# Block 0 of a two-block network as one hand-ordered TensorE stream, with expert weights spread by DMA and rotary tables made earlier

## The chip, the cores and the metric

The kernel runs on one core of a Trainium2 chip. The metric is the device time in microseconds (us) of one execution. A core has a matrix engine (PE, TensorE), three engines for elementwise work (DVE or VectorE, ACT or ScalarE, POOL or GpSimd), an engine whose queue only issues transfers here (SP), and DMA engines that move data between memory (DRAM) and the on-chip buffer. PE writes into a small accumulator memory, PSUM. Each engine takes its instructions in the order in which the program holds them, and an instruction waits on semaphores for what others must have done.

## The reference

Four batches (b) of 1024 tokens with 128 features go through two blocks; each has an attention part and a feed-forward part, both with a layer norm whose scale and shift come from a small conditioning product.

```
x = L0_attn_x                                           # 4 x 1024 x 128
sa, ca, ga, sb, cb, gb = split(silu(c0) @ wmod0)        # ga, gb kept at least 0.25 from 0
h = layernorm(x) * (1 + ca) + sa
q = softmax(heads(h Wq + bq)) * s;  k = softmax over tokens(q) * s;  v = heads(h Wv + bv)
x = x + ga * ((q @ (k^T v)) Wo + bo)                    # 16 heads of 8: linear attention
h = layernorm(x) * (1 + cb) + sb
score = sigmoid(h gate_w)                               # 16 experts in 4 groups
comb  = score, kept for the best 4 experts of the best 2 groups (score + gate_bias), else 0
x = x + gb * (sum_e comb_e * (silu(h w1_e) * (h w3_e)) w2_e + shared expert)
h = layernorm(x) * (1 + ca1) + sa1
x = x + ga1 * windowed_attention(h)                     # window 64, 16 global prefix keys
h = layernorm(x) * (1 + cb1) + sb1
for l in 0, 1:                                          # inner layers: l2-normed q and k,
    h = h + local_attention(rotary(qk-scaled h)) wo     # rotary with a scale per position,
    h = h + gelu_mlp(layernorm(h))                      # window 64, 8 heads of 64
x = x + gb1 * h
```

Each expert has 64 hidden features, so that two of them fill the 128 rows of PE. All is float32 but some constants.

## The kernel before

Activations are kept with features on the 128 partitions and tokens along the free dimension: `xT[b]` and `hT[b]` are 128x1024 for each batch. Work goes in halves of a batch (k, 512 tokens)[...].

Block 0 is written as stages, each for all batches: norms h0 (line 194), the linear attention (`linear`, lines 256 to 312), norms h1 (325), the experts (354 to 419). Block 1 follows: norms h2 (426), the windowed attention (called attention 2 here), norms h3 (646), the two inner layers with their MLPs (656 to 880), and the output. In a stage, `staggered` (line 48) runs units as generators: each new unit begins while those before it go on to their next `yield`. The order of the instructions in these stages is set by a scheduler that the kernel's framework runs over them. In attention 2 and in the attention of the inner layers the order on PE alone is the one written (`manual_schedule`); the order on the other engines is the scheduler's there too. Tiles are drawn from pools with a number of buffers per tag; a new tile waits for the readers of the one whose buffer it takes.

A layer norm (lines 139 to 163) turns four 128x128 pieces to tokens on partitions (PE transposes, tile in_h), takes statistics on DVE (bn_stats, bn_aggr), makes the inverse root on POOL (add, pow), normalizes on DVE (xh), turns back (out_h) and scales and shifts on ACT into hT.

`route(b)` (354 to 377) is the gate: 8 products of 128x16 on PE, sigmoid on ACT, then ranks by counting. `rank` (337) compares every pair of values: two DVE operations, two POOL operations (128x2048 for the experts, eq_e and gt_e) and a DVE reduction; comb, 128 tokens x 8 x 16, comes out. A route is issued before batch 0's experts and, for the next batch, ahead of the second half of each batch.

`experts` (379 to 407) is one expert pair of one half: two products h1 and h3 into PSUM (388, 390), silu on ACT (u), a product on DVE (g), then the combination weights. Those lie with tokens on partitions, but are needed along the free dimension, on all 64 rows of an expert: POOL copies them 64 times each (ce, line 399), four PE transposes turn them (cw, 402), and DVE multiplies (403). The second stage adds the pair to y in PSUM (405). A ninth unit for each half is the shared expert, with 64 rows.

The rotary tables `ab` of an inner layer are `tab` (cosines and sines with scales, 1 MB, loaded at the start) times that layer's q and k scales: eight POOL operations at the top of each layer (lines 666 to 680), before `shifted` (648 to 654) and the projections qk (692); sums with ab follow on DVE (697, 702) and POOL (709).

Transfers are issued on SP's queue, some constants on ACT's. x of batches 0 and 1 is loaded first, that of 2 and 3 while the norms h0 run, then the weights of block 0, tab and the layers' weights.

Of the kernel before, what the change touches and what calls it, by code (L numbers as in the profile page):

```python
# [19 lines left out]
F32 = mybir.dt.float32  # L20
BF16 = mybir.dt.bfloat16
AF = mybir.ActivationFunctionType
# [4 lines left out]
P = 128  # L27
# [31 lines left out]
def adaln_blocks(ctx: ExitStack, tc: tile.TileContext, a: dict, out: bass.AP):  # L59
# [21 lines left out]
    xp = ctx0.enter_context(tc.tile_pool(name="xin", bufs=2))  # L81
# [23 lines left out]
    load_x(1)  # L105
# [33 lines left out]
    def layernorm(pp, wp, src, dst, scale, bias, name, tokens=None):  # L139


        tp = tokens
        if tp is None:
            tp = pp.tile([P, 4, D], F32, tag="ln", name=f"in_{name}")
            for i in range(4):
                pe.transpose(tp[:, i, :], src[:, i * P : (i + 1) * P], ident)
# [8 lines left out]
        yield  # L155
# [3 lines left out]
        yield  # L159
        tq = pp.tile([P, BLK], F32, tag="ln", name=f"out_{name}")  # L160
# [4 lines left out]
    def ln_all(src, jscale, jbias, m, pp, wp, name, before=None, tokens=None):  # L165
        hs = [hp.tile([P, N], F32, tag=f"hT{b}", name=f"{name}{b}") for b in range(B)]

        def units():
            for b in range(B):
                for k in range(NB):  # L170
                    s = slice(k * BLK, (k + 1) * BLK)
                    if before is not None:
                        before(b, k)
                    yield layernorm(
                        pp, wp, src[b][:, s], hs[b][:, s], m[:, jscale, b : b + 1], m[:, jbias, b : b + 1], f"{name}_{b}_{k}",
                        tokens[b][:, 4 * k : 4 * k + 4, :] if tokens else None,
                    )

        staggered(units())
        return hs  # L180


    m = mods[0]
    with tc.tile_pool(name="p0", bufs=4, space=PSUM) as pp, tc.tile_pool(name="w0", bufs=3) as wp:

        def to_features(b, k):
            if k == 0 and b + 2 < B:
                load_x(b + 2)
            tp = pp.tile([P, BLK], F32, tag="tr", name=f"xtr_{b}_{k}")
            for i in range(4):  # L190
                pe.transpose(tp[:, i * P : (i + 1) * P], xin[b][:, 4 * k + i, :], ident)
            dve.tensor_copy(xT[b][:, k * BLK : (k + 1) * BLK], tp)

        hT = ln_all(xT, 1, 0, m, pp, wp, "h0", to_features, xin)
# [14 lines left out]
    ws2 = const0("ws2", [INTER, D])  # L209
    nc.sync.dma_start(out=ws2, in_=a["ws2"])  # L210
# [5 lines left out]
    tab = const("tab", [P, 2, NT, 2, DH])  # L216
    nc.sync.dma_start(out=tab, in_=a["tab"])
    wl = []
    for l in range(DEPTH):
        w = [const(f"wqkv_{l}", [P, 3, HEADS * DH]), const(f"wo_{l}", [P, 4, D]), const(f"w1_{l}", [P, 2 * HID]), const(f"w2_{l}", [P, 3, D])]  # L220
        nc.sync.dma_start(out=w[0], in_=a["wqkv"][l].rearrange("p (i c) -> p i c", i=3))
        nc.sync.dma_start(out=w[1], in_=a["wo"][l].rearrange("(c p) d -> p c d", p=P))
        nc.sync.dma_start(out=w[2], in_=a["mw1"][l])
        for j, r in enumerate(CH):
            nc.sync.dma_start(out=w[3][:r, j, :], in_=a["mw2"][l][j * P : j * P + r, :])
        wl.append(w)
# [19 lines left out]

    s_attn = float((8.0**0.5) ** -0.25)
    with (
        tc.tile_pool(name="p1a", bufs=2, space=PSUM) as pqv,
        tc.tile_pool(name="p1b", bufs=2, space=PSUM) as pmid,  # L250
        tc.tile_pool(name="p1c", bufs=2, space=PSUM) as pctx,
        tc.tile_pool(name="w1a", bufs=3) as wp,
    ):
        gabo = const("gabo", [P, B])
        dve.tensor_scalar(gabo, m[:, 2, :], cols[:, V_BO : V_BO + 1], None, ALU.mult)
        def linear(b, k, qT, cps):
            nm = f"{b}_{k}"
            ps = pqv.tile([P, 4, 2, D], F32, tag="qv", name=f"qv_{nm}")
            for i in range(4):
                t = 4 * k + i  # L260
                pe.matmul(ps[:, i, :, :], lhsT=hT[b][:, t * P : (t + 1) * P], rhs=wqv, start=True, stop=True)
            q = wp.tile([P, 4, D], F32, tag="q", name=f"q_{nm}")
            dve.tensor_tensor(q, ps[:, :, 0, :], rows[:, R_BQ : R_BQ + D].unsqueeze(1).to_broadcast([P, 4, D]), ALU.add)
            v = wp.tile([P, 4, D + 1], F32, tag="v", name=f"v_{nm}")
            pool.memset(v[:, :, D : D + 1], 1.0)
            dve.tensor_tensor(v[:, :, 0:D], ps[:, :, 1, :], rows[:, R_BV : R_BV + D].unsqueeze(1).to_broadcast([P, 4, D]), ALU.add)
# [5 lines left out]
            yield  # L272
# [5 lines left out]
            ek = wp.tile([P, 4, D], F32, tag="ek", name=f"ek_{nm}")  # L278
            act.activation(ek, q, AF.Exp)
            yield  # L280
            tp = pmid.tile([P, BLK], F32, tag="mid", name=f"qtr_{nm}")
            for i in range(4):
                pe.transpose(tp[:, i * P : (i + 1) * P], q[:, i, :], ident)
            act.copy(qT[:, k * BLK : (k + 1) * BLK], tp)
# [7 lines left out]
            cx = wp.tile([P, H0, 8], F32, tag="cx", name=f"cx_{b}")  # L292
            dve.tensor_scalar(cx, cps[:, 0:D].rearrange("p (h e) -> p h e", e=8), rs, s_attn, ALU.mult, ALU.mult)
            dve.tensor_tensor(cx, cx, bc(hm16, [P, H0, 8]), ALU.mult)
            yield
            tp = pmid.tile([P, BLK], F32, tag="mid", name=f"cxtr_{b}")
            pe.transpose(tp[:, 0:P], cx.rearrange("p h e -> p (h e)"), ident)
            cxT = wp.tile([P, D], F32, tag="cxT", name=f"cxT_{b}")
            act.copy(cxT, tp[:, 0:P])
            yield  # L300
            mps = pmid.tile([P, BLK], F32, tag="mid", name=f"mps_{b}")
            pe.matmul(mps[:, 0:D], lhsT=cxT, rhs=wo0, start=True, stop=True)
            mo = wp.tile([P, D], F32, tag="mo", name=f"mo_{b}")
            act.copy(mo, mps[:, 0:D])
            yield
            for n in range(NB):
                s = slice(n * BLK, (n + 1) * BLK)
                ops = pmid.tile([P, BLK], F32, tag="mid", name=f"o0_{b}_{n}")
                pe.matmul(ops, lhsT=mo, rhs=qT[:, s], start=True, stop=True)
                og = wp.tile([P, BLK], F32, tag="og", name=f"og_{b}_{n}")  # L310
                act.activation(og, ops, AF.Identity, bias=gabo[:, b : b + 1], scale=m[:, 2, b : b + 1])
                pool.tensor_tensor(xT[b][:, s], xT[b][:, s], og, ALU.add)

        def linear_units():
            for b in range(B):
                qT = wp.tile([P, N], F32, tag="qT", name=f"qT0_{b}")
                cps = pctx.tile([P, D + 1], F32, tag="ctx", name=f"ctx_{b}")
                for k in range(NB):
                    yield linear(b, k, qT, cps)

        staggered(linear_units())


    with tc.tile_pool(name="p2", bufs=4, space=PSUM) as pp, tc.tile_pool(name="w2a", bufs=3) as wp:
        hT = ln_all(xT, 4, 3, m, pp, wp, "h1")

    with (
        tc.tile_pool(name="p3", bufs=1, space=PSUM) as pgate,
        tc.tile_pool(name="p4", bufs=2, space=PSUM) as pp,
        tc.tile_pool(name="p4y", bufs=1, space=PSUM) as py,  # L330
        tc.tile_pool(name="w3", bufs=2) as wr,
        tc.tile_pool(name="w4", bufs=3) as wp,
    ):
        triE = tri[:, 0 : E * E].unsqueeze(1).to_broadcast([P, NT, E * E])
        triG = tri[:, E * E :].unsqueeze(1).to_broadcast([P, NT, NG * NG])
# [16 lines left out]
        combs = {}  # L352

        def route(b):

            lg = pgate.tile([P, NT, E], F32, tag="gate", name=f"gate_{b}")
# [18 lines left out]
            cb = wr.tile([P, NT, E], F32, tag="comb", name=f"comb{b}")  # L375
            dve.scalar_tensor_tensor(cb, re, float(TOPK), so, ALU.is_lt, ALU.mult)
            combs[b] = cb

        def experts(b, k, c, y):

            s = slice(k * BLK, (k + 1) * BLK)
            nm = f"{b}_{k}_{c}"
            shared = c == E // 2
            r = INTER if shared else P
            wa = ws13[:, 0, :] if shared else w1[:, c * P : (c + 1) * P]
            wb = ws13[:, 1, :] if shared else w3[:, c * P : (c + 1) * P]
            h1 = pp.tile([P, BLK], F32, tag="h1", name=f"h1_{nm}")
            pe.matmul(h1[:r], lhsT=wa, rhs=hT[b][:, s], start=True, stop=True)  # L388
            h3 = pp.tile([P, BLK], F32, tag="h3", name=f"h3_{nm}")
            pe.matmul(h3[:r], lhsT=wb, rhs=hT[b][:, s], start=True, stop=True)  # L390
            u = wp.tile([P, BLK], F32, tag="u", name=f"u_{nm}")
            act.activation(u[:r], h1[:r], AF.Silu)  # L392
            g = wp.tile([P, BLK], F32, tag="g", name=f"g_{nm}")
            dve.tensor_tensor(g[:r], u[:r], h3[:r], ALU.mult)  # L394
            if not shared:
# [5 lines left out]
                for i in range(4):  # L401
                    pe.transpose(cw[:, i * P : (i + 1) * P], ce[:, i, :, :].rearrange("p j e -> p (j e)"), ident)  # L402
# [641 lines left out]
```

## Time and profile before

| what | value |
|---|---|
| median of three runs | 1627.3 us (1626.57 to 1628.82) |
| profiled execution, its time and its span | 1627.76 us, 1626.0 us |
| mean TensorE clock granted | 0.923 of full |
| PE busy in the span | 1411.2 us (87%) |
| DVE, POOL, ACT busy | 994.8, 691.8, 646.7 us (61, 43, 40%) |
| first qv product; first y product of an expert; end of the last | 45.7; 159.8; 397.6 us |
| first scores of attention 2 read by DVE | 441.96 us |
| start of inner layers 0 and 1 (qk) | 791.5; 1207.05 us |

The profile is of one execution. A row of groups names line, engine, operation, tiles written and read, shape and count; after the bar, busy time and mean duration in ns; after the second bar, how long the engine had been idle just before these instructions, and what ended that. A timeline row gives start and length in us, and the idle time before it in square brackets. The time of an execution is a little above its span, since it also covers what lies around the recorded instructions. Ends of products on PE are modelled, so that neighbours seem to overlap: the distance between starts is the safer measure.

### The profile page before, as it was taken

To read this page: it belongs to the slowest core of one execution; us is meant where nothing else is said; L and a number is where in the kernel's file an instruction comes from. 1 tells how busy PE (TensorE), PEld (TensorE's weight loads), DVE (VectorE), ACT (ScalarE), POOL (GpSimd) and SP (SyncE) were. 2 spreads that over 40 slices of the span, in tenths; PEclk is the share of its full clock that TensorE was granted. 3 is DMA by queue.
4 is the path that set the end of the run, shared out by engine and by line. 5 is a ranking of instruction groups with operands and counts; after the bars stand their busy time and mean duration, and the time that the engine had idled before them with its cause. 6 is when DMAs were issued, how large, how long until landed. Compare 5 with 4: busy or idle time off the path is not lost. (4 is left out here: it accounts for less than half of the span.)

```text
span 1626.0 us, 34277 instructions
## 1 busy us (share of the span) xinstructions
PE 1411.2 (87%) x14132; PEld 857.4 (53%) x14132; DVE 994.8 (61%) x2258; ACT 646.7 (40%) x1395; POOL 691.8 (43%) x715
## 2 busy tenths in 40 slices
PE   4857899898699999998589999997968999998797
PEld 3634344444366767776356666664325666665433
DVE  5754844544445555554578787765447878777563
ACT  1423111211122222222176767763216767767322
POOL 2344721411402021201677777762047777777110
PEclk8966899999589999998599999998989999999899
DMA  7000000000000000000011111110001111111001
GB/s 239 22 1 1 0 0 1 1 1 0 1 2 3 3 2 3 3 3 2 0 28 31 28 29 30 25 34 4 0 1 28 24 32 27 28 31 27 11 1 52
DMA packets 24241, 30.84 MB, mean 19 GB/s; under 512 B 3243, under 2 KB 15125, under 8 KB 23957
## 3 DMA queue, kind: packets, MB, share of 16 engines
q1 hardware_dynamic: 22788, 27.10, 6.7%
q8 instruction: 112, 1.84, 0.5%
q10 hardware_dynamic: 1296, 1.54, 0.3%
q14 instruction: 45, 0.36, 0.1%
HBM read 10.56 MB, written 2.10 MB: 8 GB/s over the span
## 5 line engine op out<-in xcount | busy, mean ns | idle before, releaser
L709 POOL TENSOR_TENSOR co<-co,si 128x512 f32<-128x512 f32 x128 | 162.6, 1271 | 110.2 <-DVE si L702 110.2
L708 POOL TENSOR_TENSOR ss<-ss,nhalf 128x16 f32<-128x16 f32 x64 | 188.6, 2946 | 5.3
L772 ACT ACTIVATE pr<-s,mx,ss 128x128 f32<-128x128 f32 x512 | 186.6, 486 | 0.0
L695 ACT ACTIVATE sq<-qk 128x512 f32<-128x512 f32 x128 | 79.8, 623 | 187.2 <-issue 140.8
L692 PE MATMUL qk<-wqkv,hs_a 128*128 128x512 f32 x256 | 142.3, 645 | 8.1 <-POOL hs_a L651 7.2
L719 PE MATMUL qktr<-ident,co 128*128 128x128 f32 x512 | 82.0, 283 | 52.9 <-POOL co L711 48.2
L392 ACT ACTIVATE u<-h 128x512 f32<-128x512 f32 (+1 forms) x72 | 42.8, 596 | 193.9 <-PE h L388 188.6
L560 ACT ACTIVATE pt<-t 128x384 f32<-128x384 f32 x128 | 55.8, 488 | 156.5 <-PE t L557 156.5
L524 DVE TENSOR_REDUCE mx<-s 128x4 f32<-128x448 f32 x128 | 70.9, 616 | 74.2 <-PE s L521 74.2
L491 POOL COPY hr<-h 128x512 f32<-128x512 f32 x32 | 19.5, 613 | 217.7 <-PE vp L494 217.7
L399 POOL COPY ce<-comb 128x512 f32<-128x512 f32 x64 | 46.6, 733 | 152.7 <-PE cw L402 147.1
L767 DVE TENSOR_REDUCE mx<-s 128x4 f32<-128x512 f32 x128 | 82.4, 685 | 38.5 <-PE s L763 38.2
L697 DVE TENSOR_TENSOR co<-qk,ab 128x512 f32<-128x512 f32 x128 | 87.0, 679 | 30.0 <-ACT sq L695 24.3
L780 PEld LDWEIGHTS ptr<-ident,pr 128*128 128x128 f32 x512 | 63.5, 142 | 63.2 <-issue 50.4
L394 DVE TENSOR_TENSOR g<-u,h 128x512 f32<-128x512 f32 (+1 forms) x72 | 49.0, 683 | 74.0 <-PE h L390 70.3
L162 PE MATMUL out_h<-ident,xh_h 128*128 128x128 f32 x128 | 45.2, 436 | 53.5 <-DVE xh_h L158 50.6
L719 PEld LDWEIGHTS qktr<-ident,co 128*128 128x128 f32 x512 | 57.7, 142 | 64.1 <-POOL co L711 56.2
L702 DVE TENSOR_TENSOR si<-qk,ab 128x512 f32<-128x512 f32 x128 | 87.0, 680 | 0.9 <-POOL ab L680 0.9
L704 DVE TENSOR_REDUCE ss<-sq 128x8 f32<-128x512 f32 x128 | 86.4, 675 | 0.0
L793 PE MATMUL o<-ve,pt 128*64 128x65 f32 x1024 | 86.1, 228 | 0.0
L793 PE MATMUL o<-vs,pt 128*64 128x65 f32 x1024 | 86.1, 228 | 0.0
L405 PE MATMUL y<-g,w 128*128 128x512 f32 x128 | 72.8, 659 | 14.7 <-DVE g L403 14.7
(227 smaller groups left out, 3322.3 us busy)
## 6 DMA issues: line engine op xcount, KB each, us to landing
ve<-vs SPq DMA_DIRECT2D x120, 130.0 KB, 2.3
xin<-in_x SPq DMA_DIRECT2D x4, 512.0 KB, 4.3
out<-out SPq DMA_DIRECT2D x8, 256.0 KB, 2.4
w<-in_w SPq DMA_DIRECT2D x3, 512.0 KB, 7.5
wqkv<-in_wqkv SPq DMA_DIRECT2D x2, 768.0 KB, 6.1
tab<-in_tab SPq DMA_DIRECT2D x1, 1024.0 KB
wmod<-in_wmod ACTq DMA_DIRECT2D x1, 768.0 KB
w<-in_mw SPq DMA_DIRECT2D x2, 341.0 KB, 5.6
```

Of the source, the lines that this page charges most:

```text
L405: pe.matmul(y, lhsT=ws2 if shared else w2[:, c, :], rhs=g[:r], start=(c == 0), stop=shared)
L692: pe.matmul(ps, lhsT=kept[b, "h"][:, t * P : (t + 1) * P], rhs=wqkv[:, w, :], start=True, stop=True)
L695: act.activation(sq, ph, AF.Square)
L697: dve.tensor_tensor(co, ph, ab[:, 0, t, w, :].unsqueeze(1).to_broadcast([P, HEADS, DH]), ALU.mult)
L702: dve.tensor_tensor(si.rearrange("p h (i e) -> p h i e", i=2), ex, sn, ALU.mult)
L704: dve.tensor_reduce(ss[:, w, :], sq, AX.X, ALU.add)
L708: pool.tensor_tensor(ss, ss, nhalf[:, 0:2].unsqueeze(2).to_broadcast([P, 2, HEADS]), ALU.pow)
L709: pool.tensor_tensor(co, co, si, ALU.add)
L719: pe.transpose(tp[:, i, :], co[:, i * P : (i + 1) * P], ident)
L767: dve.tensor_reduce(mx[:, j, :], S[j], AX.X, ALU.max, negate=True)
L772: act.activation(pr[:, c, :], S[j][:, c, :], AF.Exp, bias=mx[:, j, c : c + 1], scale=rq[:, j, c : c + 1])
L793: pe.matmul(o[qs, c, :], lhsT=pt[:, c, qs], rhs=vv[:, 2 * c + j, :], start=True, stop=True)
```

## The change

Block 0 becomes one stage whose PE order is written by hand (`manual_schedule`). Its work is cut into steps: `first(b)` is norm h0, qv and context of a batch (12 steps), `second(b)` the rest of the linear attention, norm h1 and route (9), `third(b)` norm h2 of block 1 (4). `first(0)`, then `second(0)` alternating with `first(1)`, run ahead; then, for each batch, its 16 expert pairs run with side steps among them: `third` of the batch before, `second` of the next and `first` of the one after, 21, 25, 13 and 4 steps in batches 0 to 3, dealt out evenly. The products with w2 (`mixed`) follow two pairs behind (`hidden`). PSUM is shared by tags: t (transposes and all side products) with two buffers, s (hidden products) with four, m and o one each.

`spread(b, k)` replaces the copies and transposes of the combination weights: four PE transposes of comb, a copy on ACT, a 16x512 write to DRAM, and 16 DMAs of one row each, repeated into 64 partitions (128 KB written by each). They are on SP's queue. The weights are then multiplied into u on POOL, ahead of DVE's product with h3. The shared expert of a batch is done with both halves in the two halves of the partitions. The copies into xT move from DVE to ACT; all of x is loaded at the start; qv is done in quarters.

The layers' weights (4 MB) and tab are now loaded after block 0, into memory that it gives back; tab lies in a pool of attention 2, and is issued first. The two rotary tables are made in attention 2, called at its sixth step (t == 5) of batches 1 and 2. As built, POOL's order has all these 16 operations (lines 506 to 514) between the add and pow of batch 3's norm h2, ahead of attention 2's first copies of hT (hr, 583) and of its first masked keys (kg, kx, 560 and 563). tab's transfer waits for the last y product of block 0, since it takes over memory of that block.

```diff
-    xp = ctx0.enter_context(tc.tile_pool(name="xin", bufs=2))
+    xp = ctx0.enter_context(tc.tile_pool(name="xin", bufs=4))
...
-            dve.tensor_copy(xT[b][:, k * BLK : (k + 1) * BLK], tp)
...
-    tab = const("tab", [P, 2, NT, 2, DH])
-    nc.sync.dma_start(out=tab, in_=a["tab"])
...
+        tc.manual_schedule(engines={mybir.EngineType.PE}),
...
+        def mid(name, shape=(P, BLK)):
+            return ps.tile(list(shape), F32, tag="t", name=name, bufs=2)
...
+            act.copy(xT[b][:, blk(k)], tp)
...
+        def spread(b, k):
+
+            tp = mid(f"combtr_{b}_{k}")
+            for i in range(4):
+                pe.transpose(tp[0:E, i * P : (i + 1) * P], kept[b, "comb"][:, 4 * k + i, :], ident)
+            ct = wb.tile([E, BLK], F32, tag="ct", name=f"ct_{b}_{k}")
+            act.copy(ct, tp[0:E, :])
+            cd = dr.tile([E, BLK], F32, tag="cd", name=f"cd_{b}_{k}")
+            nc.sync.dma_start(out=cd, in_=ct)
+            cw = kept[b, k, "cw"] = wc.tile([P, E // 2, BLK], F32, tag="cw", name=f"cw_{b}_{k}", bufs=2)
+            for e in range(E):
+                j = e % 2 * INTER
+                nc.sync.dma_start(out=cw[j : j + INTER, e // 2, :], in_=cd[e : e + 1, :].partition_broadcast(INTER))
...
-                ce = wp.tile([P, 4, 2, INTER], F32, tag="ce", name=f"ce_{nm}")
-                w = combs[b][:, 4 * k : 4 * k + 4, 2 * c : 2 * c + 2]
-                pool.tensor_copy(ce, bc(w, [P, 4, 2, INTER]))
-                cw = pp.tile([P, BLK], F32, tag="cw", name=f"cw_{nm}")
-                for i in range(4):
-                    pe.transpose(cw[:, i * P : (i + 1) * P], ce[:, i, :, :].rearrange("p j e -> p (j e)"), ident)
-                dve.tensor_tensor(g, g, cw, ALU.mult)
...
+            act.activation(u, hh[0], AF.Silu)
+            pool.tensor_tensor(u, u, kept[b, k, "cw"][:, c, :], ALU.mult)
+            g = kept[b, k, c, "g"] = wp.tile([P, BLK], F32, tag="g", name=f"g_{nm}")
+            dve.tensor_tensor(g, u, hh[1], ALU.mult)
...
+        def first(b):
+
+            r = [(norm0, b, 0), (features, b, 0), (norm0, b, 1), (norm_out, b, 0, "h0", m, 1, 0), (features, b, 1)]
+            r += [(qv, b, 0, 0), (norm_out, b, 1, "h0", m, 1, 0), (qv, b, 0, 1), (qv, b, 1, 0), (qv, b, 1, 1)]
+            return r + [(context, b, 0), (context, b, 1)]
+
+        def second(b):
+
+            r = [(turn_context, b), (join_context, b), (attended, b, 0), (attended, b, 1)]
+            r += [(norm_in, b, 0, "h1"), (norm_in, b, 1, "h1"), (norm_out, b, 0, "h1", m, 4, 3), (norm_out, b, 1, "h1", m, 4, 3)]
+            return r + [(route, b)]
...
+        run(first(0))
+        run(braid(second(0), first(1)))
+        for b in range(B):
+            side = third(b - 1) if b else []
+            if b + 1 < B:
+                side = side + second(b + 1)
+            if b + 2 < B:
+                side = side + first(b + 2)
+            if b == 0:
+                for k in range(NB):
+                    run([(spread, b, k)])
+            units = [(k, c) for k in range(NB) for c in range(E // 2)]
+            shared_hidden(b)
+            for i in range(len(units) + 2):
+                if i < len(units):
+                    hidden(b, *units[i])
+                take = max(0, (i + 1) * len(side) // len(units) - i * len(side) // len(units)) if i < len(units) else 0
+                at = i * len(side) // len(units)
+                run(side[at : at + take])
+                if i >= 2:
+                    mixed(b, *units[i - 2])
+                if i == len(units) - 1 and b + 1 < B:
+                    spread(b + 1, 0)
+            if b + 1 < B:
+                spread(b + 1, 1)
+        run(third(B - 1))
...
+        tab = wb.tile([P, 2, NT, 2, DH], F32, tag="tab", name="tab", bufs=1)
+        nc.sync.dma_start(out=tab, in_=a["tab"])
...
+            if t == 5 and 0 < b <= DEPTH:
+                rotary(tab, abs_[b - 1], b - 1)
...
-            ab = wt.tile([P, 2, NT, 2, DH], F32, tag="ab", name=f"ab_{l}")
...
+            ab = abs_[l]
```

## The prediction

> **What bounds the kernel now.** I first read the page's second part, its PE and PEclk rows: 40 slices of 40.65 us.
>
> ```profile
> PE   4857899898699999998589999997968999998797
> PEclk8966899999589999998599999998989999999899
> ```
>
> PE holds the kernel nearly everywhere; the loose slices are the first four, the eleventh (406 to 447 us) and the starts of later norms. The change touches the first eleven and the two layer starts (slices 20 and 30). So next come the busy times by stretch:
>
> ```profile
> core 0: us, PE busy (x) PEld busy (x) DVE busy (x) ACT busy (x) POOL busy (x), PEclk, DMA share, GB/s
> ...
> 100.00:150.00 50.00, 36.22 (x130) 23.66 (x130) 28.52 (x101) 15.48 (x20) 18.84 (x19) 0.63 0.00 1
> 150.00:200.00 50.00, 37.59 (x113) 19.59 (x114) 39.31 (x48) 7.50 (x11) 32.35 (x24) 0.82 0.00 0
> ...
> 250.00:300.00 50.00, 50.00 (x157) 22.45 (x155) 21.75 (x32) 9.92 (x17) 9.20 (x15) 1.00 0.00 1
> ...
> 400.00:450.00 50.00, 30.30 (x155) 15.75 (x155) 24.42 (x98) 7.57 (x11) 21.16 (x32) 0.56 0.00 0
> ```
>
> Where the experts run undisturbed (250 to 300 us) PE is full at full clock, with DVE at 44% and POOL at 18%. Around them it has holes, and works at a lowered clock. The timeline of PE there prices an expert unit:
>
> ```profile
> 253.60 0.60 PE L402 MATMUL cw<-ident,ce 128*128 128x128 f32 x4
> 254.04 1.02 PE L388 MATMUL h<-h,w 128*128 128x512 f32 x2
> 254.90 1.02 PE L390 MATMUL h<-h,w 128*128 128x512 f32 x2
> 255.76 1.02 PE L405 MATMUL y<-g,w 128*128 128x512 f32 x2
> 256.62 0.60 PE L402 MATMUL cw<-ident,ce 128*128 128x128 f32 x4
> ```
>
> From start to start: a 512-column product 0.86 us, four transposes 0.44, a unit 3.02. The hole before the experts, in the groups of 127 to 160 us:
>
> ```profile
> L345 POOL TENSOR_TENSOR eq_e<-eq_e,tri 128x2048 f32<-128x2048 f32 x1 | 6.5, 6498 | 5.7 <-DVE eq_e L342 5.7
> L347 POOL TENSOR_TENSOR gt_e<-gt_e,eq_e 128x2048 f32<-128x2048 f32 x1 | 4.5, 4493 | 0.1
> L360 ACT ACT_TABLE_LOAD x3 | 3.8, 1283 | 10.7 <-DVE comb L376 6.9 <-PE gate L358 3.8
> L349 DVE TENSOR_REDUCE rank_e<-gt_e 128x128 f32<-128x2048 f32 x1 | 2.3, 2285 | 4.5 <-POOL gt_e L347 4.5
> ```
>
> A batch's routing is a serial chain over POOL and DVE, 22 us from sigmoid (done 133.2) to comb (154.96); sigmoid and silu take turns in ACT's table, 1.283 a load. Last, the layer starts:
>
> ```profile
> 798.49 0.69 DVE L697 TENSOR_TENSOR co<-qk,ab 128x512 f32<-128x512 f32 x1 [5.34 <-POOL ab L680]
> 1207.05 5.49 PE L692 MATMUL qk<-wqkv,hs_a 128*128 128x512 f32 x6 [7.18 <-POOL hs_a L651]
> ```
>
> Both wait for POOL's rotary products: eight of 128x256 at 0.726, four of 128x512 at 1.488, four at 1.666, so 18.4 us in both layers.
>
> **What the Trainium skill says.** "Perfetto Trace Analysis", Optimization Strategy, advises interleaving regimes whose busiest engine differs; the table above has such regimes. "TensorE: Matmul & The Clock Gate", What's actually happening: the clock halves after an idle window of about 3.4 us and needs a busy one to recover; in the trace h passes lasted 0.96 us at 131 us and start 0.43 apart at 250, so every stall costs more than its length. "GPSIMD Engine Reference", 4.1 Engine selection: two-input elementwise work is about twice as slow there; POOL took 1.271 for 128x512, DVE 0.683.
>
> **The change, part by part.**
>
> *PE's work.* Block 0 after: 128 hidden products x 0.855 = 109.4; 64 mixed = 54.7; shared 16+8 = 20.5; eight kinds of transposes (x, two of each norm except h0's input, q, comb), 32 of each at 0.107 = 27.4; qv, context, o0 and gate 31. Together 243 us. Before it was 267: the 256 cw transposes cost 27.4, the new comb transposes 3.4. Before, this work and its holes took from 18.3 us to the first scores' maximum at 441.96. The gain is bounded by the holes.
>
> *The start.* Only batch 0's norms stand ahead of its first qv: about 23 us instead of 45.7. Softmax, context, o0 and two h1 norms are a serial chain of one batch (each half: stats 1.2, aggregate 0.6, POOL add and pow 1.26, xh 1.6, transposes 0.5, Identity 0.78, and hand-overs); gate(0) ends near 57, sigmoid 58. Routing takes the same 22: comb at 80 (155 before). Then, new: four transposes and a copy 1.1, the write to DRAM and the first broadcast, two DMAs on end. For these the nearest row is ve, 130 KB, 2.3 us to landing; with issue 7.4 in all, and a POOL product, so the first g is at 90. By unit 3 PE is warm: 96.
>
> *Spread weights.* Per unit it removes 4 transposes (0.44 PE), a POOL copy (0.733) and a DVE product (0.686), and adds a POOL product of 1.27 between silu and g. POOL has 64 x 0.54 = 34 us more in all, in a block where it was 18 to 65% busy: hidden, except when a rank block stands ahead on POOL. The 128 broadcasts (128 KB each, 16.8 MB) have one half's expert time, 8 x 2.57 + side work, about 30 us, per 2 MB. "SBUF — State Buffer", Door 1, has 196 GB/s measured for 64 partitions, so an estimate of 10.7 us per half; no run here shows it. Bounds: 0 (hidden) to 128 x what exceeds 1.9 us each. I take 0, since comb is ready well ahead for batches 1 and 2.
>
> *Batches.* Experts, shared and comb transposes are 47 PE us per batch; first(b) is 7.7, second 4.5, third 1.7. From t=96: batch 0, rest of it 50 plus stalls 15; batch 1, 60 plus 17.5; batch 2, 53 plus 24.6; batch 3, 45. The last y ends near 360. The stalls: PE is now one written order, so any late side step stops the experts too. The q softmax (reduce, subtract on POOL, exp, sum, reciprocal, scale, exp: about 9) starts at unit (1,6), and its transposes come at unit (1,7): 5 in batches 0 and 1. A rank block (DVE 2.3 + 4.2, POOL 5 + 4.5, in order) holds up POOL's u x cw and DVE's g by more than the two units that the four s buffers cover: 6 and 4.5. The rest are norms, 4 and 8. In batch 2, route(3) is the last side step, after unit (1,7); the comb transposes of batch 3 follow it on PE at once, so 18.6 of the 20 us chain lie bare, with 3 for other waits and 3 for the cold clock. Bounds for all stalls: 22 (start of batch 3 alone) to twice 57.
>
> *Boundary.* h2 norms of batches 0 to 2 are hidden among experts. But POOL's built order puts all 16 rotary products between the norm operations of batch 3's h2 and ahead of the kg and kx products that the first scores need, though the source calls them in batches 1 and 2 of that attention. The first waits for tab (1 MB), now issued after block 0: if like xin and w (512 KB in 4.3 to 7.5), about 8.8 after the last POOL product, T = 357.5. Rotary with the norms between until T+29, five copies and kx until T+36, first scores T+38.5 = 396, instead of 442: gain 45; I take 43 for clock loss. Without rotary in the way it would be about T+22. Behind them PE's out_h of batch 3, q and k wait. The layer weights (4 MB) load behind tab, with 390 us until layer 0.
>
> *Layer starts.* Rotary is done: 5.3 off at layer 0, 7.2 at layer 1 less what co waits next, so 10 together.
>
> Sum: 43 + 10 = 53 off the profiled execution's 1627.76 (span 1626.0 plus 1.8 around it, 0.5 above the median 1627.3): 1574.5.
>
> **Rivals.**
> 1. *Overlap is better.* The soft stalls hide, as four s buffers and three u and g tiles give slack; only start, route(3) and boundary remain: 33 less, 1543. For it: DVE at 44% in mid-experts. Against: strict order on DVE and POOL with rank blocks of 5 to 6.5 us.
> 2. *Side steps choke DVE.* A full batch gives it 51 us in 61; if stalls double except route(3), 30 more: 1605. For: DVE then is past 80%. Against: before, it ran 39 of 50 at 150 to 200.
> 3. *Rotary does not hold the boundary* (the move does what it says; tab lands earlier or POOL has room): 16 less, 1558. Against: the built order.
> 4. *Slower: broadcasts bind.* Experts wait on cw through DRAM. From 90 us to the end that cancels the gain (360 + 53 = 413) there are 323 us for 128: past 2.5 us each in series (52 GB/s) the kernel is slower; at 3 us, 384, so 61 more: 1636. For: every broadcast repeats 2 KB rows into 64 partitions only. Against: ve's 130 KB lands in 2.3 with latency[...]; 239 GB/s were moved in the first slice.
> 5. *Nothing gained*: a stall somewhere eats all; I see no place for it.
>
> **How the numbers follow.** Likeliest 0.47, 1574.5 (its own range 1560 to 1590); rival 1 0.16; rival 2 0.18; rival 3 0.13; rival 4 0.05; rest 0.01. From 1538 (rival 1 and a little) to 1606 (rival 2) holds eight in ten. A change under 0.2%, 3.3 us, is about what measurement can't tell from none. Faster 0.94, same 0.01, slower 0.05.
>
> **What would show it.** First y near 91 (159.8 before). PE idle of 15 to 20 us once, before the last batch's experts, released by comb; PE stalls of 4 to 6 around unit (1,7) of batches 0 and 1. Last y of block 0 near 360. In the next 30 us POOL full of ab products, PE idle with norm and kx behind POOL; first scores near 397. DVE's first co of layer 0 and PE's first qk of layer 1 without waits on POOL. Broadcasts landing in 2 to 5 us, no wait on cw past the first half of batch 0 and batch 3. Wrong if u x cw waits for DMAs in every half (rival 4), if the last y is before 330 (1) or after 385 (2), or if rotary is found later (3).

## The result, and the profile after

The changed kernel takes 1599.86 us (median of four runs, 1596.70 to 1604.01), before the change 1627.58 (four runs); the ratio is 0.9831, 95% interval 0.9807 to 0.9855. That is 27.7 us faster. The forecast was 1574.5, 53 us faster: the direction held and the time lies in the range of 1538 to 1606, but 25 us of the expected gain did not come. The profiled execution took 1599.65 us, span 1597.7.

Where the two profiled executions differ, stage by stage, as distances between events in each:

| stretch | before | after | change |
|---|---|---|---|
| start to first y product | 159.8 | 96.2 | -63.6 |
| first y to DVE's last read of y, block 0 | 238.0 | 286.2 | +48.2 |
| that to the first scores of attention 2 | 44.2 | 35.7 | -8.5 |
| first scores to layer 0's first qk | 349.5 | 353.0 | +3.5 |
| layer 0's first qk to layer 1's | 415.6 | 405.8 | -9.8 |
| layer 1's first qk to the end | 418.9 | 420.8 | +1.9 |
| sum | 1626.0 | 1597.7 | -28.3 |

The experts' stretch is longer, since the rest of block 0 now lies in it; together with the start it gained 15.4. The page's second part of the changed kernel, PE and its clock in slices of 39.9 us:

```profile
PE   5596888776699999997689999997978999999797
PEclk8688899988599999998799999998989999999899
```

No slice of block 0 (the first ten) has PE above 8 but one. Busy times of the changed kernel by stretch: the experts of batches 0, 1, 2 and 3, then the boundary.

```profile
core 0: us, PE busy (x) PEld busy (x) DVE busy (x) ACT busy (x) POOL busy (x), PEclk, DMA share, GB/s
96.00:169.00 73.00, 58.85 (x185) 31.08 (x184) 38.93 (x96) 26.28 (x36) 39.09 (x31) 0.86 0.11 37
169.00:257.00 88.00, 71.41 (x225) 36.33 (x225) 45.11 (x123) 30.66 (x44) 44.22 (x36) 0.90 0.16 49
257.00:334.00 77.00, 57.66 (x172) 26.30 (x171) 31.87 (x80) 19.33 (x30) 39.67 (x30) 0.87 0.17 56
334.00:382.00 48.00, 47.90 (x129) 20.97 (x128) 17.80 (x43) 13.56 (x21) 23.39 (x24) 1.00 0.29 91
382.00:418.00 36.00, 16.50 (x71) 6.00 (x69) 7.29 (x28) 2.75 (x4) 29.39 (x33) 0.59 0.32 114
```

PE idles 14.2, 16.6, 19.3 and 0.1 us in the four batches, 50 in all. It is busy 235.8 us for what the forecast priced at 208. Its clock, as a mean over idle and busy time, stood at 0.86 to 0.90 in three of them, and only batch 3, whose side steps are few, ran at full clock. What PE waited for between 96 and 382 us (microseconds in total, times, longest):

```profile
PE combtr L379 <- DVE comb L373: 18.9, 1, 18.9
PE qtr L304 <- DVE q L292: 8.7, 3, 4.9
PE y L420 <- DVE xT L424: 8.5, 2, 8.1
PE out_h L161 <- DVE xh_h L155: 6.3, 4, 3.5
PE y L422 <- DVE g L414: 5.6, 3, 3.7
```

First the bare routing of batch 3, then the softmax, then a wait for xT, which stands behind DVE's g; that g waits for a u that stands behind a ranking block on POOL (eq_e, 125.11 to 131.58 us). At the boundary, the timeline of POOL and the layer starts in the timelines of DVE and PE:

```profile
386.11 0.72 POOL L506 TENSOR_TENSOR ab<-tab,rows 128x256 f32<-128x256 f32 x1 [4.91 <-DMA tab<-in_tab]
...
402.18 3.05 POOL L514 TENSOR_SCALAR ab<-ab 128x512 f32<-128x512 f32 x2
405.30 1.72 POOL L583 COPY hr<-hT 128x512 f32<-128x512 f32 x3
```

```profile
773.85 0.69 DVE L775 TENSOR_TENSOR co<-qk,ab 128x512 f32<-128x512 f32 x1 [1.31 <-ACT sq L773]
```

```profile
1176.86 5.37 PE L770 MATMUL qk<-wqkv,hs_a 128*128 128x512 f32 x8 [2.33 <-DVE hs_a L747]
```

Rotary products, with a norm's four small operations among them, fill POOL for 19 us at the boundary, and the layers no longer wait for them (5.34 and 7.18 before; the waits of 1.31 and 2.33 that are left are for ACT and DVE).

### The profile page after: what moved, and what is told of

Its sections match the earlier page's. It is cut to its first block, busy times and chain, and to the rows that moved or that the text cites. A ratio compares the mean times of both kernels' runs of the same rounds, so it can differ in the third digit from the quotient of the medians.

```text
span 1597.7 us, 33824 instructions
## 1 busy us (share of the span) xinstructions
PE 1366.6 (86%) x13908; PEld 829.3 (52%) x13908; DVE 940.7 (59%) x2198; ACT 668.8 (42%) x1418; POOL 730.3 (46%) x715
## 5 line engine op out<-in xcount | busy, mean ns | idle before, releaser
L412 POOL TENSOR_TENSOR u<-u,cw 128x512 f32<-128x512 f32 x64 | 81.1, 1270 | 99.2 <-ACT u L411 56.0
L408 PE MATMUL h<-hT,w 128*128 128x512 f32 x256 | 125.1, 615 | 0.0
L583 POOL COPY hr<-hT 128x512 f32<-128x512 f32 x32 | 19.5, 612 | 222.0 <-PE vp L586 221.9
L414 DVE TENSOR_TENSOR g<-u,h 128x512 f32<-128x512 f32 x64 | 43.7, 684 | 89.8 <-POOL u L412 89.7
L411 ACT ACTIVATE u<-h 128x512 f32<-128x512 f32 x64 | 38.2, 597 | 119.7 <-PE h L408 118.1
L408 PEld LDWEIGHTS h<-hT,w 128*128 128x128 f32 x256 | 49.7, 197 | 64.1 <-issue 59.6
```

Of the source, the lines that this page charges most:

```text
L408: pe.matmul(h, lhsT=w[:, c * P : (c + 1) * P], rhs=hT[b][:, blk(k)], start=True, stop=True)
L412: pool.tensor_tensor(u, u, kept[b, k, "cw"][:, c, :], ALU.mult)
```

## The experiments

Times are medians of four runs each; the changed kernel is 1599.86. Its runs scatter by some 7 us, and the intervals of five single edits (routing, spread earlier, ranking, softmax, clock) overlap its own, so what such an edit is worth is not settled by time alone; the profiles' distances say where it is. Two things there are not of the edits. The start ran in two ways, 4 to 5 us apart, which the last section shows; a profile with the longer one is said to have a cold start. And from the first scores of attention 2 to the end the builds that keep the rotary products out of the layers took from 1176.5 to 1183.3 us.

### Rotary products: at the layers, or late

The first run undoes this part: tab is still loaded after block 0, but each layer makes its own table again.

```diff
-            if t == 5 and 0 < b <= DEPTH:
-                rotary(tab, abs_[b - 1], b - 1)
...
-            ab = abs_[l]
+            ab = wt.tile([P, 2, NT, 2, DH], F32, tag="ab", name=f"ab_{l}")
+            rotary(tab, ab, l)
```

> The changed kernel with one part undone: the rotary products stand at the top of each inner layer again (tab is still loaded after block 0). My theory (they hold the boundary, because POOL's order has them ahead of batch 3's norms and the first masked keys): the first scores come about 16 us earlier, counted from the last y of block 0 (20 instead of 36 us), and the layers' starts lose 10 again, so about 6 us faster than the changed kernel, 1594. Rival (the boundary is not held by them, moving them is a plain gain): the boundary stays at 36 us and the kernel is 10 us slower, 1610.

1599.54 us (ratio 0.9834, 0.9819 to 0.9848): no change. The boundary, last read of y to first scores, is 25.3 us instead of 35.7, and DVE and PE wait again at the two layers, 5.34 and 7.17 us. So both halves of the theory hold in kind, but its 6 us did not come: the boundary's price was 10.4, not 16, about the same as the gain at the layers. This part of the change is worth nothing as built.

The second holds tab's buffer and each table until the keys of attention 2 have come far enough:

```diff
+            if t == 5 and b == 0:
+                pool.tensor_copy(hold[:, 0, 0, 0, 0:PREFIX], kept[1, "kg"][:, 0, :])
+                tab = wb.tile([P, 2, NT, 2, DH], F32, tag="tab", name="tab", bufs=1)
+                nc.sync.dma_start(out=tab, in_=a["tab"])
             if t == 5 and 0 < b <= DEPTH:
+                for i in range(2):
+                    pool.tensor_copy(abs_[b - 1][:, i, :, :, 0:PREFIX], kept[b + 1, "kg"][:, 0:NT, :].unsqueeze(2).to_broadcast([P, NT, 2, PREFIX]))
                 rotary(tab, abs_[b - 1], b - 1)
```

> The changed kernel with the rotary products really inside the second attention: tab takes a buffer that is held until batch 1's masked keys, and each layer's table is held by a small copy from the next batch's keys, so POOL's order has them in the middle of that attention. My theory: the boundary is 16 us shorter and the layers' starts keep their gain: 1584. Rival (POOL's blocks of 9 us hold up the attention's hr and kx products by as much): no better than 1594.

1589.60 us (0.9782, 0.9763 to 0.9801), 10.3 faster, where the theory had 16. The boundary is 25.4, the layers keep their gain, and first to last scores of attention 2 took 296.4 us against 296.6: POOL's blocks cost nothing there.

### The routing of batch 3

```diff
-            if b + 1 < B:
+            if b == 2:
+                side = second(3) + [(run, [])] + side + [(run, [])] * 2
+            elif b + 1 < B:
                 side = side + second(b + 1)
```

> The changed kernel with one order changed: among batch 2's experts the nine steps that end with the routing of batch 3 stand first, then the four of batch 1's norm h2. My theory (18.9 us of PE idle before batch 3 is the tail of that routing): of its 22 us chain about 13 more are covered, and PE's clock stays up, so about 15 us faster, 1585. Rival (the chain is slower among experts, as DVE and POOL serve both, so it is late anyway): 5 us or less.

1591.83 us (0.9792, 0.9770 to 0.9814), 8 faster: between theory and rival (in the profile 9.9 behind the first y). The 18.9 us wait is gone, but another came, in the timelines of PE and of DVE:

```profile
313.93 1.11 PE L161 MATMUL out_h<-ident,xh_h 128*128 128x128 f32 x4 [12.09 <-DVE xh_h L155]
```

```profile
310.11 2.29 DVE L348 TENSOR_REDUCE rank_e<-gt_e 128x128 f32<-128x2048 f32 x1 [8.39 <-POOL gt_e L346]
312.32 0.40 DVE L155 TENSOR_SCALAR xh_h<-in_h,mv_h 128x128 f32<-128x128 f32 x1
```

DVE stands at rank_e, which waits for POOL's two blocks, and the norm's xh stands behind it; PE, in its written order, stops the experts for that norm. A step moved out of a stall is only worth what the next step in the order lets it be.

### The spread of weights earlier

```diff
-                if i == len(units) - 1 and b + 1 < B:
+                if i == (12, 14, 15)[min(b, 2)] and b + 1 < B:
```

> The changed kernel with the spread of the next batch's first half issued at the 13th pair of batch 0 and the 15th of batch 1 instead of the last. POOL waits 15 us for the first weights at the starts of batches 1 and 2. My theory (PE works on through most of that wait, at shared experts and side steps): 3 us a batch at most, 1594 to 1600. Rival (the DRAM round trip is what slows batches 0 and 1): 10 a batch, 1580.

1594.42 us (0.9803, 0.9789 to 0.9818), within the theory. POOL no longer waits for the first weights of batches 1 and 2 (15.2 and 15.1 us in the changed kernel), but in two places it idles 13.7 and 13.5 us all the same, with no u to multiply, and the last y comes only 1.6 earlier in the profile, 1.2 of it there at the first y already; most of the rest lies behind the first scores (3.1 us), where the edit changes nothing. So the long waits on the transfer mostly covered time in which POOL had nothing else to do.

### Ranking on DVE

```diff
+            on = dve if n == E else pool
-            pool.tensor_tensor(eqf, eqf, tri_b, ALU.mult)
+            on.tensor_tensor(eqf, eqf, tri_b, ALU.mult)
```

and the addition after it likewise.

> The changed kernel with the two 128x2048 operations of each expert ranking on DVE instead of POOL (2.3 us each there by the rows of that size, against 6.5 and 4.5). My theory (the rank blocks on POOL, in order ahead of u x cw, are the longest soft stalls: 8.08 us in batch 0, 3.7 in batch 1, and half of the bare chain before batch 3; each also lowers PE's clock for some us): routing is 6 us shorter, those stalls fall to 2 or 3 each; 12 to 16 us faster than the changed kernel, 1584 to 1588, with the first y about 6 earlier. Rival (DVE's longer block of five such operations holds up g as much as POOL's held up u): only the 12 us at both bare chains, that is the start and batch 3, or less than 6 in all.

1593.52 us (0.9799, 0.9782 to 0.9815), 6 faster, where the theory had 12 to 16. The bare chain before batch 3 fell from 18.9 to 14.5 us. The first y came only 1.6 earlier, at 94.6, but this profile had a cold start: the two others that had one without this edit show 99.8 and 100.0, so here the theory's 6 came nearly whole. Batch 0's wait for xT did not fall: 10.6 instead of 8.1, and 3.2 came before it. The rival is right inside the experts: DVE's block holds up g as POOL's held up u.

### Weights turned on PE again

```diff
-            pool.tensor_tensor(u, u, kept[b, k, "cw"][:, c, :], ALU.mult)
+            pool.tensor_copy(ce, bc(w, [P, 4, 2, INTER]))
+            cw = mid(f"cw_{nm}")
+            for i in range(4):
+                pe.transpose(cw[:, i * P : (i + 1) * P], ce[:, i, :, :].rearrange("p j e -> p (j e)"), ident)
             g = kept[b, k, c, "g"] = wp.tile([P, BLK], F32, tag="g", name=f"g_{nm}")
             dve.tensor_tensor(g, u, hh[1], ALU.mult)
+            dve.tensor_tensor(g, g, cw, ALU.mult)
```

`spread` is empty in this build.

> The changed kernel with the weights spread as before the change: POOL copies, four PE transposes a pair, and a DVE product, in the new order; no transfer through DRAM. My theory (the DMA way takes 24 us of PE work off and costs 7 to 10 at the start and about 3 at each later batch): PE gets 24 more at an effective clock of 0.9, so 27, less 7 at the start and 3 for each of three batches: 11 slower, 1611. Rival 1 (the DMA round trip eats what it saves): within 4 of 1600. Rival 2 (the soft stalls have room for the transposes, so they cost nothing): faster, 1590.

1611.97 us (0.9917, 0.9891 to 0.9943), 12 slower. The figure is the theory's, but not by its terms. First to last y took 314.2 us instead of 285.5, so 28.7 more; the first y came 5.7 earlier; and the boundary was 25.4 instead of 35.7, because in this build POOL's order happens to have the rotary products after the keys, as its timeline shows:

```profile
426.26 4.03 POOL L559 TENSOR_TENSOR kx<-k,hm 128x512 f32<-128x512 f32 x4 [1.01 <-DVE k L554]
430.48 1.40 POOL L502 TENSOR_TENSOR ab<-tab,rows 128x256 f32<-128x256 f32 x2
```

Without that accident the spread by DMA is worth about 23 us in this order (28.7 - 5.7), the largest part of the change that one edit undoes.

### Softmax given time

```diff
+            if b == 1:
+                side = first(2)[-2:] + side
             if b + 2 < B:
-                side = side + first(b + 2)
+                side = side + (first(2)[:-2] if b == 0 else first(b + 2))
```

> The changed kernel with the two context steps of batch 2 moved from the end of batch 0's experts to the head of batch 1's, so that their softmax has time. My theory (4.86 us of PE idle at the last pair of batch 0 plus the lowered clock after it): 5 to 7 faster, 1593 to 1595. Rival (the next thing, the weights through DRAM, is late at the same place): 2 or less.

1605.09 us (0.9864, 0.9847 to 0.9882): 5 slower by time, neither theory nor rival. Batch 0's experts, first y to its last read, fell from 72.5 to 63.6 us; batch 1's rose from 88.5 to 97.9, with waits of 4.8 us for a norm (3.5 before the edit), 4.7 for v and 3.6 for g. The same DVE and POOL work now stands closer together there; that this is the cause was not tested. So the stall moved, and all four batches together took 286.7 us instead of 286.2. The profile (1600.82 us) had a cold start, its first y 3.8 later, and shows no loss behind it; why the other three runs took 3 to 6 us more is open.

### Three and four edits together

> The changed kernel with three of the edits at once: rotary products late, routing of batch 3 first, spread early. They work at different places, so if my reading of the places is right their gains (10, 8, 5) add: 1577. If one only uncovers the next, less than 15 in all: 1585 or more.

1581.04 us (0.9724, 0.9708 to 0.9740): 18.8 faster than the changed kernel where the single gains add to 24. The profile had a cold start (first y 3.6 later, at steps that no edit touches); behind the first y it is 21.1 shorter, where the three single profiles add to 24.6. So the gains add but for 3.5 us.

> Rotary late, routing of batch 3 first, spread early, and the ranking's two large operations on DVE. Beside the three of the run before (1581), the 12.1 us stall that the reordered batch 2 showed (its norm waits behind ranking's 6.5 and 4.5 us blocks on POOL) should shrink and the start gain 4: 1572. Rival (DVE's block takes POOL's place there too): only the start, 1577 or more.

1576.29 us (0.9689, 0.9673 to 0.9704). The start gained, with the first y at 89.7; the wait in batch 2 went only from 12.1 to 11.1, and behind the first y the profile is no shorter than with three edits (1482.1 and 1480.4 us), so there the rival holds.

### The clock after stalls

Products that nobody reads fill part of three stalls.

```diff
+        def idle(n):
+            d = mid("idle", (P, 2 * D))
+            for _ in range(n):
+                pe.matmul(d, lhsT=ident, rhs=wqv, start=True, stop=True)
...
+        def late_context(b, k):
+            idle(8)
+            context(b, k)
...
+                side[-1] = (late_context, 2, 1)
...
+                if b == 0 and i == 10:
+                    idle(14)
...
+                    if b == 2:
+                        idle(37)
                     spread(b + 1, 0)
```

> The changed kernel with products that nobody reads put on PE into its three longest stalls among the experts: 14 of 256 columns (6 us) before the 8.08 us one of batch 0, 8 (3.4 us) before the 4.86 us one, 37 (16 us) before the 18.9 us one. They do nothing but keep PE active. My theory (the missing time in block 0 is PE working at a lowered clock after stalls: 236 us busy for 208 us of work, while the idle time was as predicted): the clock stays up after these three, 2 to 3 us each, so 6 to 9 faster, 1591 to 1594, with more work on PE. Rival (the clock in the records costs nothing, the busy time grew for another reason, such as waits inside the rows): 1600 or slower.

1592.54 us (0.9802, 0.9777 to 0.9826), 7.3 faster with 25 us more work on PE. Busy times around the first two stalls and behind the third (which ends at 329.84 and 325.47 us), of the changed kernel and then of this run:

```profile
126.00:140.00 14.00, 5.92 (x9) 2.20 (x8) 5.88 (x6) 0.75 (x2) 12.50 (x4) 0.63 0.00 0
160.00:168.00 8.00, 6.37 (x21) 4.29 (x22) 2.22 (x6) 1.79 (x3) 0.00 (x0) 0.58 0.00 0
330.00:334.00 4.00, 4.00 (x8) 1.61 (x7) 0.00 (x0) 0.57 (x1) 0.00 (x0) 0.50 0.04 8
```

```profile
126.00:140.00 14.00, 11.94 (x38) 7.43 (x37) 5.85 (x8) 0.60 (x1) 12.95 (x5) 0.88 0.01 1
160.00:168.00 8.00, 8.00 (x36) 3.95 (x37) 1.77 (x5) 4.19 (x6) 0.00 (x0) 1.00 0.06 18
325.60:329.60 4.00, 4.00 (x11) 1.61 (x10) 0.23 (x1) 0.58 (x1) 0.00 (x0) 0.57 0.04 8
```

The clock is up at the first two. Batch 0 is 3.0 us shorter (69.5 instead of 72.5): the work from the end of the first stall to the next qv took 0.8 less, that from the end of the second to the shared expert 2.2. PE's work at half clock there fell from 13.6 to 6.8 us, worth 3.4. That is the mechanism of the theory, in size too. The third filling ended 3.0 us before its stall did, and the clock still fell: behind the stall it is low in both rows, and batch 2 is only 0.4 us shorter. Of the 8.5 us between the two profiled executions 3.8 lie among the experts, 4.7 elsewhere, where the edit changes nothing.

### A faster version

The four edits, and batch 1's norm h2 moved to batch 3's experts; then the same with batch 0's two fillings.

```diff
-                side = second(3) + [(run, [])] + side + [(run, [])] * 2
+                side = second(3) + [(run, [])] * 7
+            elif b == 3:
+                side = third(1) + side
```

> The run with four edits, and batch 1's norm h2 taken out of batch 2's experts and put among batch 3's, where only four steps stood. My theory (the 11.1 us stall left in batch 2 is that norm's xh, queued behind the ranking of batch 3, and the ranking itself is in time): about 9 faster than the four edits, 1567. Rival (the ranking's end is as late, and the stall moves to the comb transposes): 4 or less, 1572 or more.

1573.59 us (0.9670, 0.9652 to 0.9688). The 11.1 us wait is gone, one of 3.0 is left in batch 2, and first to last y fell from 279.2 to 271.5. So the theory holds there, 7.7 of its 9. The time reads like the rival's (2.7 faster, not settled), but this profile had a cold start, 4.9 us longer than the one before.

> The run before with the two fillings of batch 0 (14 and 8 unread products ahead of its stalls of about 9 and 5 us). If a stall costs PE's clock for some us after it, another 4 to 6 off, 1562; if the fillings only helped by chance, no change or slower by what they take, 1567 to 1570.

1565.18 us (0.9623, 0.9607 to 0.9639), 8.4 less, and the fastest here: 61 us below the kernel before the change, run beside it, and 35 below the changed kernel. In the profiles batch 0's experts are 1.9 shorter than in the run before, and 4.9 of the difference lies in the start, ahead of the fillings: cold in the run before, not in this one. So the fillings' own worth is some 2 us by profile; how often each kernel started cold in the other runs is not known.

## Why the prediction was right or wrong

- **Start.** Right in its end, partly by luck. The first qv came at 18.6 (forecast 23), but gate(0) ended at 59.0 (57), so the chain between them was longer than forecast, and routing took 24 us (22). Then comb(0) came at 83.4 (80), the first g at 92.3 (90), the third pair and with it the first y at 96.2, which is the 96 from which the sum went on. Only the check at the end, which named 91 for the first y, forgot that y follows two pairs behind.
- **Stalls.** Right in sum: 54 us forecast (57 less 3 for the clock), 50.2 idle. The bare routing was 18.9 (18.6), the softmax 4.9 and 5.1 (5 and 5), the ranking 8.1 and 3.7 (6 and 4.5).
- **PE's work in the batches: the step that failed.** "Batch 0, rest of it 50 plus stalls 15; batch 1, 60 plus 17.5; batch 2, 53 plus 24.6; batch 3, 45" makes 265 us, with 3 for the cold clock in one place. The four took 73, 88, 77 and 48 us, 21 more, though PE idled 4 less: it was busy 28 us longer than the 208 of this sum. Part of that is the clock. Its record has only full and half clock in it, and between 96 and 382 us it shows eight stretches at half clock. Four of them, with what PE worked there, and the sum of all eight:

```profile
core 0: us, PE busy (x) PEld busy (x) DVE busy (x) ACT busy (x) POOL busy (x), PEclk, DMA share, GB/s
112.10:115.50 3.40, 3.40 (x6) 1.34 (x5) 2.09 (x9) 1.92 (x3) 1.79 (x4) 0.50 0.00 0
129.20:139.40 10.20, 5.15 (x6) 2.01 (x7) 3.44 (x3) 0.00 (x0) 9.30 (x4) 0.50 0.00 0
...
248.70:255.50 6.80, 5.64 (x19) 4.07 (x20) 1.79 (x5) 1.45 (x3) 0.00 (x0) 0.50 0.01 2
313.50:334.00 20.50, 4.16 (x8) 1.73 (x9) 7.17 (x5) 0.57 (x1) 10.97 (x2) 0.50 0.01 2
sum 57.90, PE 33.39 PEld 16.84 DVE 24.11 ACT 7.91 POOL 26.50; mean PE 4.17 PEld 2.11 DVE 3.01 ACT 0.99 POOL 3.31
```

  PE worked 33.4 us at half clock, which at full clock would have been 16.7. The other 24.5 us at half clock were idle and cost nothing; 16 of them lie in the bare stall before batch 3, the only place that the forecast charged. It cited "TensorE: Matmul & The Clock Gate", What's actually happening, and concluded that every stall costs more than its length, but did not carry this to the shorter stalls; this trace agrees with the conclusion, with half clock after nearly every stall of 2 to 8 us. The filling run shows the mechanism at two stalls (3.0 us); that all 17 would come back is not shown. The other 11 of the 28 are work priced too low: at full clock the batches need some 219 us. Batch 3 was put at 45 where the forecast's own prices, 47 and a norm of 1.7, make 48.7, and took 48; the rest is spread over batches 0 to 2.
- **Spread by DMA.** Hidden, as forecast, but for one thing: "comb is ready well ahead for batches 1 and 2" looked at comb and not at the place of the spread, behind the last pair. POOL waited 15 us for them at the starts of batches 1 and 2, where the forecast expected no wait on cw, but PE little: bringing it forward gave 5.4 by time, of which the profile places 0.4 among the experts. Broadcasts landed in 2.8 to 3.9 us, so rival 4 is out. They were issued 0.6 us apart on SP, so a half took about 10 us, near the 10.7 of the estimate; whether the issue or the transfer set that was not told apart.
- **Boundary.** The 36 us are as forecast (35.7), and rotary does hold them. "Without rotary in the way about T+22" was wrong: in both runs without it there the first scores come 27.3 us after the last POOL product of block 0, which is the forecast's T. Q, k and scores of batch 0 follow one another there, with two products of 512 columns in 2.08 us instead of 1.02, so at half clock. So rival 3 would have given 10, not 16.
- **Layer starts.** 9.8 of 10.
- **Attention 2 and the end** took 3.5 and 1.9 more than before, which no step had. Between first and last scores the changed kernels took 294.8 to 299.9 us, before 293.6; why is open.
- **Rivals.** The time lies outside the likeliest case's own range (1560 to 1590) and near rival 2's 1605, but stalls did not double: the clock, low prices and the later stages made the difference, so the number came near that rival's for other reasons than its own.
- **Slips.** 442 less 396 is 46, not 45; rival 1's 33 us lead to 1541.5, not 1543; and rival 4's 61 us count from the point where the gain is gone, which makes about 1689, not 1636. The h passes at 131 us are given by length and those at 250 by distance: in distance they are 0.86 and 0.43 apart. None of this moves the likeliest figure by more than 1 us.

## What to carry to other kernels

When work of several engines is woven into one written PE order, price each stall twice: its length, and the work that follows it at a lowered clock. Count the clock only where work is done: low clock under a stall costs nothing, so a mean over a stretch overstates it. Before an edit is judged by a few us, see whether the two profiles ran alike where it changes nothing. A step that leaves a stall is worth what the next late step allows, so follow the order on DVE and POOL, with their longest blocks, before moving anything. And where a scheduler places an operation on another engine, read the built order: the call's place in the source says nothing, and an unrelated edit can move it.

## What the runs showed of the hardware that was not expected

- The clock fell behind a busy PE too, and behind a stall of 2.1 us (201.9 to 204.1, half clock from 204.3 to 207.7), shorter than the idle window of about 3.4 us that the forecast cites. While batch 0's gate ran (16 passes of 16 columns, 109.57 to 111.67 us in the changed kernel) PE was recorded busy, and then:

```profile
108.00:112.00 4.00, 3.93 (x24) 2.78 (x23) 3.37 (x15) 2.80 (x4) 2.27 (x3) 1.00 0.17 60
112.00:116.00 4.00, 4.00 (x7) 1.67 (x6) 2.09 (x9) 2.02 (x3) 2.39 (x4) 0.57 0.00 0
```

  The gate alone does not do it: in the profile of ranking on DVE the same 16 passes ran from 107.97 to 110.07 us, and the clock stayed full until 130.3. What sets it off is open.

- One DVE instruction on two on-chip operands, 0.68 us at 64.08, took 4.41 at 71.97 while POOL worked on eq_e from 69.36 to 75.83. "SBUF — State Buffer", Who interferes with whom, says that a DVE instruction with two on-chip inputs and a POOL instruction that reads there lock each other out of a shared port pair; this trace agrees, as DVE's ended 0.55 us after POOL's, and it is dearer than what the forecast took for gt_e (4.2 in such company, 2.3 alone). The lock may also be why POOL took 6.5 us for eq_e and 4.5 for gt_e of the same size: eq_e began 0.2 us after DVE's own gt_e, which ran 2.3; that was not tested.

```profile
64.08 0.68 DVE L292 SCALAR_TENSOR_TENSOR q<-q,sm 128x512 f32<-128x512 f32 x1
...
71.97 4.41 DVE L292 SCALAR_TENSOR_TENSOR q<-q,sm 128x512 f32<-128x512 f32 x1
```

- The same start ran in two ways. In four of the thirteen profiles of the new order (ranking on DVE, softmax, three edits, and the first of the faster version) PE's clock between 56 and 64 us was 0.50, in the other nine 0.90 to 0.93, with the same steps on PE up to there. The first y came at 99.8 and 100.0 us in the cold ones, at 95.0 to 96.3 in the others; with ranking on DVE at 94.6 in both cold ones and 89.7 in both others (90.5 where PE turns the weights). So the way a run starts is worth 4 to 5 us, as much as several of the edits. That may be why the changed kernels' runs scatter by up to 9 us, and those of the kernel before by 2 to 4; what decides it is open.
